# A four-layer graph network on one core: one-hot products in place of a gather, marks moved to another engine, a fused subtraction

## The chip, the cores and the metric

The kernel runs on one core of one Trainium2 chip. The metric is the device time of one execution in microseconds (us), as the median of several runs. A profile is one further execution, recorded by the hardware profiler; its times are microseconds, and those of single instructions are nanoseconds (ns). The engines of the core are TensorE (PE in the profile, with its weight loads as PEld), VectorE (DVE), ScalarE (ACT), GpSimd (POOL) and the queue of SyncE (SP), which here only starts transfers.

## The reference, cut to what matters

There are 16 graphs of 1024 nodes with 64 features each. Four layers follow one another, each of the form x = x + f(relu(layernorm(x)), adj). Layers 0, 1 and 3 multiply by the weighted adjacency matrix. Layer 2 is the costly one: for every node and every feature it takes the 0.25, 0.5 and 0.75 quantiles over the node's neighbours (after a rule that removes some neighbours), adds them with weights 0.25, 0.5 and 0.25, and puts the sum through a small network:

```python
h = maximum(layernorm(x), 0)
valid = dilate(adj, mask) > 0                    # which neighbours count
agg = sum(w * quantile(h over the valid neighbours, t)
          for t, w in ((.25, .25), (.5, .5), (.75, .25)))
y = relu((h + agg) @ W1 + b1) @ W2 + b2
x = x + y * mask
```

The layernorm is (x - mean(x)) / sqrt(var(x) + 1e-5) over the 64 features.

## The kernel before, in words

A graph's 1024 nodes lie on 128 partitions in 8 blocks. The main path is `direct_path`. It sorts the nodes of each graph by their number of neighbours, so that blocks of nodes with similar counts share one sorting network. The position of each node in this order is `pos`, and the node at each position is `node`. Six streams work on the graphs:

- `adjacency` loads the adjacency matrix, transposes it on TensorE, counts and removes neighbours, writes a matrix of keys to DRAM, and works out `pos` and `node` (L1062 to L1085).
- `layers` computes layers 0 and 1 and the normalised input `h2` of layer 2, and writes it to DRAM as the table `h_d`. Layers 0 and 1 each hold a product of 16 instructions with the transposed adjacency (`messages`, L883); layer 1 is followed by eight in-place copies on ScalarE (L1228) that sum the degrees.
- `neighbour_lists` fetches the rows of keys in sorted order with indirect transfers (L1100), finds the neighbours with max-of-eight instructions on VectorE (L1119, L1133), and makes the lists `index`.
- `gathers` fetches the features of the neighbours from `h_d` with one indirect transfer for each slot and block (L1294), 124 a graph, into the tiles `raw0` to `raw4`, one for each group of blocks, of which there is a single buffer each.
- `sorts` runs the sorting networks on VectorE (L1327), adds up the weighted quantiles in `agg` (L1344 to L1350), and sends `agg` to DRAM from SP's queue (L1355). The order of its rows is the sorted one.
- `tail` brings the aggregate back into the order of the nodes: eight indirect transfers on GpSimd read the rows of `agg_d` at `pos` into `res` (L1366). `paired` then adds `h2` and `res` while it transposes them on TensorE (L891), ScalarE copies the sum (L893), and the rest of layer 2 (L1375 to L1381) and layer 3 (L1403 to L1419) follow.

The order of all instructions is fixed when the program is built. A planner in Python holds a clock for each engine (`clk.dve`, `clk.pe`, `clk.act`, `clk.pool`), to which each piece of work adds planned costs. A stream gives the time from which it wants to continue; the planner takes the first stream of the list whose time has come by `clk.dve`. `after` adds to the clocks and returns when a result should be there. Each engine then works through its own list strictly in order, so a waiting instruction holds up everything behind it on that engine.

`gate` (L919 to L926) ties GpSimd to this plan. It is called ahead of every few gathers. If more than 3 us of planned VectorE time have gone since the last mark, a one-element memset is issued on VectorE (L923), and GpSimd copies that element (L925); so GpSimd doesn't go on before VectorE has reached the mark.

`preln` (L850 to L865) is the layernorm, used four times a graph: a sum (L854), its scaling to a mean (L855), the subtraction (L856), a square on ScalarE (L857), a second sum (L859), a root on ScalarE (L860), a reciprocal (L862), a multiplication (L863), and a relu on ScalarE (L864).

The pool `lists` has two buffers of every tile unless said otherwise. Tiles with one tag share these buffers.

Of the kernel before, what the change touches and what calls it, by code (L numbers as in the profile page):

```python
# [7 lines left out]
F32 = mybir.dt.float32  # L8
F16 = mybir.dt.float16
BF = mybir.dt.bfloat16  # L10
I32 = mybir.dt.int32
# [3 lines left out]
ALU = mybir.AluOpType  # L15
AX = mybir.AxisListType

P = 128
C = 64
NB = 8  # L20
N = 1024
# [30 lines left out]
J_ID, J_BIG, J_OFF, J_ST, J_ROW, J_ONE, J_PI, J_NI, J_NEG, J_END = 0, 128, 256, 384, 896, 1920, 2048, 2176, 2184, 2312  # L52
# [680 lines left out]
def direct_path(ctx: ExitStack, tc: tile.TileContext, t: dict, out: bass.AP, flag):  # L733
# [3 lines left out]
    nc = tc.nc  # L737
    x_in, adj, nodemask = t["x"], t["adj"], t["nodemask"]
    B = x_in.shape[0]

    const = ctx.enter_context(tc.tile_pool(name="const", bufs=1))
    loads = ctx.enter_context(tc.tile_pool(name="loads", bufs=2))
    graph = ctx.enter_context(tc.tile_pool(name="graph", bufs=1))
    nodes = ctx.enter_context(tc.tile_pool(name="nodes", bufs=2))
    lists = ctx.enter_context(tc.tile_pool(name="lists", bufs=2))
# [10 lines left out]
    ch = const.tile([P, J_END], F16, name="eh")  # L756
# [4 lines left out]
    stair, pidx = ch[:, J_ST:J_ST + N // 2], ch[:, J_PI:J_PI + P]  # L761
    nid = ch[:, J_NI:J_NI + NB]
    jrow, onerow = ch[0:1, J_ROW:J_ROW + N], ch[0:1, J_ONE:J_ONE + P]
# [45 lines left out]
    nc.gpsimd.dma_start(mask8, nodemask.rearrange("b (i p) -> (b i) p", p=P))  # L809
    maskf = lists.tile([B * NB, P], F32, tag="ab", name="maskf")  # L810
    nc.vector.tensor_copy(maskf, mask8)
# [10 lines left out]
    clk = Clock()  # L822

    def after(dve=0.0, pe=0.0, act=0.0, lat=0.3):

        clk.dve += dve
        at = clk.dve
        if pe:
            clk.pe = at = max(clk.pe, at) + pe
        if act:  # L830
            clk.act = at = max(clk.act, at) + act
        return at + lat

# [15 lines left out]
    def preln(u, x, ha):  # L849

        s = nodes.tile([P, 4, NB], F32, name="stat")
        xc = mid(u, [P, NB, C])
        sq = mid(u, [P, NB, C])
        nc.vector.tensor_reduce(s[:, 0], x, AX.X, ALU.add)  # L854
        ts(s[:, 1], s[:, 0], 1.0 / C, None, op0=ALU.mult)  # L855
        tt(xc, x, s[:, 1, :, None].to_broadcast([P, NB, C]), ALU.subtract)  # L856
        act(sq, xc, AF.Square)  # L857
        yield after(1.5, act=0.65, lat=1.2)
        nc.vector.tensor_reduce(s[:, 2], sq, AX.X, ALU.add)  # L859
        act(s[:, 3], s[:, 2], AF.Sqrt, bias=eps, scale=1.0 / C)  # L860
        yield after(0.7, act=1.0, lat=1.5)
        nc.vector.reciprocal(s[:, 2], s[:, 3])  # L862
        tt(xc, xc, s[:, 2, :, None].to_broadcast([P, NB, C]), ALU.mult)  # L863
        act(ha[:, :, :C], xc, AF.Relu)  # L864
        yield after(0.9, act=0.65)  # L865
# [20 lines left out]
    def paired(hs, dst):  # L886

        p = bank()
        for q in range(4):
            for e, h in enumerate(hs):  # L890
                nc.tensor.matmul(p[:, q * P:(q + 1) * P], h[:, 2 * q:2 * q + 2, :].rearrange("p u c -> p (u c)"), identf,  # L891
                                 start=e == 0, stop=e == len(hs) - 1)
        nc.scalar.copy(dst, p)  # L893
        clk.pe = max(clk.pe, clk.dve) + 2.0 * len(hs)
        clk.act = max(clk.act, clk.pe) + 0.7
# [15 lines left out]
    def even(v, u):  # L911

        return v.rearrange("c (q u p) -> c u q p", u=2, p=P)[:, u]


    marks = []
    slots = const.tile([1, 8], F32, name="mark")
    opened = const.tile([1, 2], F32, name="gate")

    def gate():  # L920
        if not marks or clk.dve > marks[-1] + 3.0:
            k = len(marks)
            nc.vector.memset(slots[:, k % 8:k % 8 + 1], 0.0)  # L923
            clk.dve += 0.15
            nc.gpsimd.tensor_copy(opened[:, k % 2:k % 2 + 1], slots[:, k % 8:k % 8 + 1])  # L925
            marks.append(clk.dve)  # L926

# [13 lines left out]
    def adjacency(b):  # L941
# [108 lines left out]
        for q in range(2):  # L1050
            spread = lists.tile([P, 4, P], F32, tag="ab", name="spread")
            tt(spread, identf[:, None, :].to_broadcast([P, 4, P]),
               key[:, 4 * q:4 * q + 4, None].to_broadcast([P, 4, P]), ALU.mult)
            nc.tensor.matmul(p[:, q * 512:(q + 1) * 512], onesf, spread.rearrange("p j m -> p (j m)"),
                             start=True, stop=True)
        over = nodes.tile([P, NB], F32, name="over", bufs=1)
        for i in range(NB):
            sink = lists.tile([P, N], F16, tag="ab", name="sink")
            act(sink, p, AF.Sign, bias=neg[:, i:i + 1], accum_out=over[:, i:i + 1])
        yield after(1.6, pe=1.3, act=10.5, lat=2.0)  # L1060
        pos = nodes.tile([P, NB], I32, name="pos", bufs=5)
        ts(pos, over, 0.5, 511.5, op0=ALU.mult, op1=ALU.add)  # L1062
# [5 lines left out]
        nc.vector.tensor_copy(ph, pi)  # L1068
        low = lists.tile([P, NB, P], F16, tag="ab", name="low")
        tt(low, pidx[:, None, :].to_broadcast([P, NB, P]), ph[:, 0, :, None].to_broadcast([P, NB, P]), ALU.is_equal)  # L1070
# [13 lines left out]
        node = nodes.tile([P, NB], I32, name="node", bufs=3)  # L1084
        nc.vector.tensor_copy(node, p[:, :NB])  # L1085
        clk.dve += 0.1
        g.update(pos=pos, node=node, m=m, keys_d=keys_d)
        done.add(("keys", b))
# [222 lines left out]
    def sorts(b):  # L1311
        g = state[b]
        agg_d = dram.tile([N, C], F32, name="agg_d")
        agg = nodes.tile([P, NB, C], F32, name="agg", bufs=1)
        for k, (b0, n, cap, low, *_) in enumerate(GROUPS):
# [18 lines left out]
            o = sum(len(_wanted(kk, ll)) * m for _, m, kk, ll, *_ in GROUPS[:k])  # L1334
            wv = g["wts"][:, o:o + len(places) * n].rearrange("p (q i) -> p q i", i=n)

            half = nodes.tile([P, C], F32, name="half", bufs=1)
# [15 lines left out]
            yield clk.dve  # L1353
        yield clk.dve + 2
        nc.sync.dma_start(agg_d.rearrange("(i p) c -> p i c", p=P), agg)  # L1355
        g.update(agg_d=agg_d, agg_at=clk.dve + 4)
        done.add(("sorts", b))


    def tail(b):  # L1360
        g = state[b]
        x, ha, adjt_d = g["x"], g["h2"], g["adjt_d"]
        yield g["agg_at"]
        res = nodes.tile([P, NB, C], F32, name="res", bufs=1)
        for i in range(NB):
            nc.gpsimd.indirect_dma_start(res[:, i, :], None, g["agg_d"],  # L1366
                                         bass.IndirectOffsetOnAxis(ap=g["pos"][:, i:i + 1], axis=0))
        clk.pool = max(clk.pool, clk.dve) + 10.5
        yield clk.pool + 3.5
        rt = mid(1, [P, 512])  # L1370
        paired((ha, res), rt)
        h1 = big(1, [P, N])
# [4 lines left out]
        y = per_node(bank(), h1, w22, 8, b22)  # L1377
        yield after(0, pe=6.5, act=2.1) + 6.0
        o = mid(1, [P, NB, C])
# [51 lines left out]
    programs = [_program(*group[2:]) for group in GROUPS]  # L1431
    edge = lists.tile([1, 2, C], F32, tag="ab", name="edge")
    nc.vector.memset(edge[:, 0], 0.0)
# [64 lines left out]
def _constants():  # L1498
# [25 lines left out]
    eh[p, J_ST + p] = 2050  # L1524
    eh[0, J_ROW:J_ROW + N] = np.arange(N) - 2047
    eh[0, J_ONE:J_ONE + P] = 1
# [76 lines left out]
```

## Time and profile before

| what | value |
|---|---|
| time, median of 3 runs | 3631.67 us (3631.34 to 3632.71) |
| time of the profiled execution | 3640.35 us |
| its span | 3638.5 us |
| VectorE busy | 3072.9 us, 84% of the span |
| GpSimd busy | 2651.7 us, 73% |
| TensorE busy | 1993.7 us, 55% |
| ScalarE busy | 1410.6 us, 39% |
| mean granted TensorE clock | 0.698 of full speed |

The span is the time from the first to the last recorded instruction. Dispatch of an instruction isn't counted as busy, so an engine with many short instructions is fuller than its busy share says; between two indirect transfers GpSimd shows an idle time "<-issue" of about 0.3 us. A row of the groups gives the line, the engine and operation, output <- inputs with shapes, the count, then busy time in us, mean duration in ns, and the idle time in front of these instructions with what ended it. A row of waits gives who waited for whom: the total in us, how many times, and the longest. One product with fp32 operands leaves two matmul records.

### The profile page before, as it was taken

The page shows a single profiled execution, that of the slowest core. Times are in us where ns is not written, and L with a number is a line of the kernel's source. Part 1 is how long each engine was busy: PE and PEld are TensorE (multiplying, and loading weights), DVE is VectorE, ACT ScalarE, POOL GpSimd, SP SyncE. Part 2 cuts the span into 40 slices and gives each one's busy share as a digit, 9 for nine tenths or more (in the row PEclk, how much of TensorE's full clock was granted, in tenths as well). Part 3 has the DMA queues.
Part 4 walks back from the last instruction along what each step waited for, and adds up shares of the span by engine and source line. Part 5 has one row for each costly group of instructions (what it writes and reads, how often), then busy time and mean ns, then how long its engine had stood idle before and what let it go on. Part 6 is the DMA issues. An engine that isn't in the chain of part 4 may idle for free.

```text
span 3638.5 us, 31082 instructions
## 1 busy us (share of the span) xinstructions
PE 1993.7 (55%) x7587; PEld 923.9 (25%) x7587; DVE 3072.9 (84%) x7539; ACT 1410.6 (39%) x2770; POOL 2651.7 (73%) x2777
## 2 busy tenths in 40 slices
PE   6564565746666565746555556765646565550303
PEld 3222222323222222322222222232322322220101
DVE  3497989989898998989798997989898888989662
ACT  5444434344444344353444435443443534330000
POOL 1187787878777787877777787787778777777881
PEclk9676767676676676767676667667667776765555
DMA  2324243342424334151433425243332525232211
GB/s 90 120 62 122 60 129 102 112 129 62 152 66 133 95 109 128 49 184 44 145 81 111 122 72 166 55 134 89 126 109 63 167 56 157 49 123 52 74 27 57
DMA packets 237344, 362.38 MB, mean 100 GB/s; under 512 B 126848, under 2 KB 128496, under 8 KB 237152
## 3 DMA queue, kind: packets, MB, share of 16 engines
q1 hardware_dynamic: 156912, 255.00, 20.2%
q0 software_dynamic: 80096, 104.70, 14.1%
q8 instruction: 62, 1.02, 0.1%
q14 instruction: 130, 1.06, 0.1%
q10 hardware_dynamic: 144, 0.59, 0.0%
HBM read 245.30 MB, written 114.81 MB: 99 GB/s over the span
## 4 chain that ended last, share of the span: by engine, by line
DVE 61%; POOL 11%; issue 11%; DMA 7%; PE 5%; ACT 3%; SPq 0%; DVEq 0%; POOLq 0%; ACTq 0%
DVE raw L1327 16%; DVE other L1327 16%; POOL raw L1294 10%; DVE most L1133 6%; PE pt L883 4%; DVE found L1119 4%; DMA raw<-h_d,index 3%; DVE agg L1346 2%; ACT adjt L1228 2%; DMA k<-keys_d,node 2%; DVE k L1128 2%; DVE nb L948 2%; DVE found L1134 1%; DVE k L1130 1%; DVE gone L1007 1%
## 5 line engine op out<-in xcount | busy, mean ns | idle before, releaser
L1294 POOL DMA_INDIRECT raw<-h_d,index x1984 | 2165.2, 1091 | 558.8 <-issue 498.8
L1327 DVE TENSOR_TENSOR other<-raw 128x512 f32<-128x512 f32 (+11 forms) x816 | 536.4, 688 | 162.5 <-DMA raw<-h_d,index 132.9
L883 PE MATMUL pt<-adjt,ha 128*65 128x512 f32 (+1 forms) x1024 | 492.7, 643 | 91.0 <-DVE ha L1215 68.7
L995 PE MATMUL pt<-eh,nbt 128*128 128x512 f16 (+3 forms) x1024 | 236.6, 379 | 310.2 <-ACT nbt L984 309.7
L1327 DVE TENSOR_TENSOR raw<-other 128x512 f32<-128x512 f32 (+10 forms) x464 | 356.7, 791 | 5.6
L955 PE MATMUL pt<-ef,a 128*128 128x128 f32 x1024 | 205.2, 356 | 220.2 <-ACT adjt L957 136.2
L925 POOL COPY gate<-mark 1x1 f32<-1x1 f32 x462 | 156.4, 339 | 225.0 <-DVE mark L923 217.3
L1133 DVE MAX8 most<-k 128x8 uint16<-128x1024 uint16 x208 | 255.4, 1228 | 7.2
L962 ACT ACTIVATE nb<-nb 128x512 f16<-128x512 f16 x256 | 159.2, 624 | 255.6 <-DVE nb L948 149.6
L883 PEld LDWEIGHTS pt<-adjt,ha 128*65 128x65 f32 (+1 forms) x1024 | 149.9, 150 | 417.6 <-issue 403.3
L955 PEld LDWEIGHTS pt<-ef,a 128*128 128x128 f32 x1024 | 155.6, 183 | 321.6 <-ACT adjt L957 173.9
L995 PEld LDWEIGHTS <-nbt 128*128 128x128 f16 x1024 | 110.4, 120 | 436.0 <-ACT nbt L984 340.7
L1327 DVE TENSOR_TENSOR raw<-other,raw 128x640 f32<-128x640 f32 (+3 forms) x448 | 216.5, 494 | 5.0
L884 ACT COPY big<-pt 64x1024 f32<-64x1024 f32 (+1 forms) x32 | 32.3, 1008 | 476.8 <-PE pt L883 476.8
L1327 DVE TENSOR_TENSOR raw<-raw,other 128x128 f32<-128x128 f32 (+7 forms) x496 | 211.7, 436 | 6.0
L1403 PE MATMUL tm<-at,ha 128*64 128x512 f32 x512 | 175.3, 786 | 74.5 <-DMA at<-adjt_d 74.5
L1002 ACT ACTIVATE gone<-pt,sf 128x512 f16<-128x512 f32 x256 | 161.4, 683 | 124.5 <-DVE sf L976 95.3
L1029 PE MATMUL pt<-eh,gone 128*128 128x128 f16 x1024 | 127.2, 253 | 145.2 <-DVE gone L1007 77.8
L1327 DVE TENSOR_TENSOR other<-other,raw 128x128 f32<-128x128 f32 (+4 forms) x448 | 200.6, 459 | 3.8
L1119 DVE MAX8 found<-k 128x8 f32<-128x1024 f16 x128 | 156.3, 1221 | 51.6 <-DMA k<-keys_d,node 51.6
L891 PE MATMUL pt<-ef,res 128*128 128x128 f32 x128 | 38.9, 399 | 291.9 <-DMA res<-agg_d,pos 291.9
L1034 ACT ACTIVATE nb<-pt 128x1024 f16<-128x1024 f32 x120 | 122.4, 1020 | 164.9 <-PE pt L1032 89.2
(192 smaller groups left out, 4373.6 us busy)
## 6 DMA issues: line engine op xcount, KB each, us to landing
a<-in_adj_dram SPq DMA_DIRECT2D x64, 1024.0 KB
adjt_d<-adjt SPq DMA_DIRECT2D x64, 1024.0 KB
at<-adjt_d SPq DMA_DIRECT2D x128, 512.0 KB
keys_d<-nb SPq DMA_DIRECT2D x64, 512.0 KB
raw<-h_d,index POOLq DMA_INDIRECT x1984
x<-in_x_dram SPq DMA_DIRECT2D x16, 256.0 KB
h_d<-h SPq DMA_DIRECT2D x16, 256.0 KB
agg_d<-agg SPq DMA_DIRECT2D x16, 256.0 KB
```

Source lines behind the costliest of these rows:

```text
L883: nc.tensor.matmul(p[p0:p0 + n, s], h[:, j, :n], adjt[:, j, s], start=j == 0, stop=j == NB - 1)
L925: nc.gpsimd.tensor_copy(opened[:, k % 2:k % 2 + 1], slots[:, k % 8:k % 8 + 1])
L955: nc.tensor.transpose(p[:, u * P:(u + 1) * P], a[:, j * P:(j + 1) * P], identf)
L962: act(nb[:, i, s], nb[:, i, s], AF.Copy, accum_out=mn[:, q, i:i + 1])
L995: nc.tensor.matmul(p[:, o:e], nbt[:, j, :], stair[:, :e - o], start=j % 4 == 0, stop=j % 4 == 3 and j != i)
L1002: act(gone[:, i, s], p[:, s], AF.Abs, bias=sf[:, 2 + q, i:i + 1], scale=2.0)
L1029: nc.tensor.matmul(p[:, d], gone[:, j, i * P:(i + 1) * P], big_i, start=False, stop=j == 4 * q + 3 and i // 4 != q)
L1119: nc.vector.max(out=eights[0], in_=src)
L1133: nc.vector.max(out=most, in_=less.bitcast(U16))
L1294: nc.gpsimd.indirect_dma_start(raw[:, s, i * C:(i + 1) * C], None, h_ds[b % 3], bass.IndirectOffsetOnAxis(ap=g["index"][:, at:at + 1], axi ...
L1327: tt(view(two[to], *((i, vi) if greater else (j, vj)), w), view(two[s], i, vi, w), view(two[u], j, vj, w), ALU.max if greater else ALU.min)
L1403: nc.tensor.matmul(p[q * C:(q + 1) * C, :], ha[:, j, :], even(ats[j], q), start=j == 0, stop=j == NB - 1)
```

## The change

Three parts are changed, and one rearrangement of buffers goes with them.

*Marks.* A mark is now a one-element copy on ScalarE. It is issued inside `after`, whenever work on ScalarE has been planned and more than 3 us of planned ScalarE time have gone since the last mark; its planned time is kept. `gate` issues no mark any more: it looks among the last 20 marks for the latest with a planned time more than 1 us before GpSimd's, and, unless that one was used before, lets GpSimd copy it.

*Aggregate.* `agg` stays in SBUF. From the positions a tile `place` is kept (the node's number less 2047, as the row `iota` counts). `tail` builds for each of the 8 blocks two 128x512 matrices `hot` on VectorE, which hold 1 where the number of the column's node equals that of the row's. TensorE multiplies the block of `agg` by them and adds into one PSUM tile, which already holds the transposed `h2`. ScalarE copies the sum. `sorts` of a graph now waits, in the plan, until the aggregate of the graph before has been brought back.

*Layernorm.* The scaling of the sum and the subtraction become one instruction, x + sum * (-1/64).

*Buffers.* The tiles of tag "ab" share the buffers of "nbt"; `pos` has one buffer instead of five, and `place` has five.

```diff
+    def mark():
+        if not marks or clk.act > marks[-1][0] + 3.0:
+            t = slots[:, len(marks) % 32:len(marks) % 32 + 1]
+            nc.scalar.copy(t, eps[:1])
+            clk.act += 0.2
+            marks.append((clk.act, t))
+
+    def gate():
+        due = [m for m in marks[-20:] if m[0] < clk.pool - 1.0]
+        if due and gates[-1:] != due[-1:]:
+            gates.append(due[-1])
+            nc.gpsimd.tensor_copy(opened[:, len(gates) % 2:len(gates) % 2 + 1], due[-1][1])
...
     def after(dve=0.0, pe=0.0, act=0.0, lat=0.3):
...
             clk.act = at = max(clk.act, at) + act
+            mark()
         return at + lat
...
-        ts(s[:, 1], s[:, 0], 1.0 / C, None, op0=ALU.mult)
-        tt(xc, x, s[:, 1, :, None].to_broadcast([P, NB, C]), ALU.subtract)
+        nc.vector.scalar_tensor_tensor(xc, s[:, 0, :, None].to_broadcast([P, NB, C]), -1.0 / C, x, op0=ALU.mult, op1=ALU.add)
...
-    def gate():
-        if not marks or clk.dve > marks[-1] + 3.0:
-            k = len(marks)
-            nc.vector.memset(slots[:, k % 8:k % 8 + 1], 0.0)
-            clk.dve += 0.15
-            nc.gpsimd.tensor_copy(opened[:, k % 2:k % 2 + 1], slots[:, k % 8:k % 8 + 1])
-            marks.append(clk.dve)
...
-            spread = lists.tile([P, 4, P], F32, tag="ab", name="spread")
+            spread = lists.tile([P, 4, P], F32, tag="nbt", name="spread")
...
+        place = nodes.tile([P, NB], F32, name="place", bufs=5)
+        ts(place, p[:, :NB], -2047.0, None, op0=ALU.add)
...
     def sorts(b):
...
+            while b and ("back", b - 1) not in done:
+                yield None
...
-        yield clk.dve + 2
-        nc.sync.dma_start(agg_d.rearrange("(i p) c -> p i c", p=P), agg)
-        g.update(agg_d=agg_d, agg_at=clk.dve + 4)
+        g.update(agg=agg)
...
     def tail(b):
...
-        yield g["agg_at"]
-        res = nodes.tile([P, NB, C], F32, name="res", bufs=1)
-        for i in range(NB):
-            nc.gpsimd.indirect_dma_start(res[:, i, :], None, g["agg_d"],
-                                         bass.IndirectOffsetOnAxis(ap=g["pos"][:, i:i + 1], axis=0))
-        clk.pool = max(clk.pool, clk.dve) + 10.5
-        yield clk.pool + 3.5
+        yield clk.dve + 1.0
+
+        agg = g["agg"]
+        p = psum.tile([P, 512], F32, name="tm")
+        for q in range(4):
+            nc.tensor.matmul(p[:, q * P:(q + 1) * P], ha[:, 2 * q:2 * q + 2, :].rearrange("p u c -> p (u c)"), identf,
+                             start=q == 0, stop=False)
+        clk.pe = max(clk.pe, clk.dve) + 2
+        for k in range(NB):
+            for u in range(2):
+                hot = lists.tile([P, 512], F32, name="hot")
+                ts(hot.rearrange("p (q m) -> p q m", m=P), even(iota, u), g["place"][:, k:k + 1], None, op0=ALU.is_equal)
+                nc.tensor.matmul(p[u * C:(u + 1) * C, :], agg[:, k, :], hot, start=False, stop=k == NB - 1)
+            yield after(0.8, pe=1.5) - 1.5
+        done.add(("back", b))
         rt = mid(1, [P, 512])
-        paired((ha, res), rt)
+        nc.scalar.copy(rt, p)
...
-        yield after(0, pe=6.5, act=2.1) + 6.0
+        yield after(0, pe=6.5, act=3.2) + 6.0
...
-    eh[0, J_ROW:J_ROW + N] = np.arange(N) - 2047
+    eh[:, J_ROW:J_ROW + N] = np.arange(N) - 2047
```

## The prediction

> **What bounds the kernel now.** I read the page's busy shares first, then the same by slices and by stages (busy time in windows), then who waited for whom on VectorE and GpSimd, in the steady stretch from 440 to 3300 us and at the end, and last the rows of the operations concerned. Busy shares of the page, and two of its rows of 40 slices of 91 us:
>
> ```profile
> PE 1993.7 (55%) x7587; PEld 923.9 (25%) x7587; DVE 3072.9 (84%) x7539; ACT 1410.6 (39%) x2770; POOL 2651.7 (73%) x2777
> ...
> DVE  3497989989898998989798997989898888989662
> POOL 1187787878777787877777787787778777777881
> ```
>
> VectorE (DVE) is the busiest, with a slow start and end. By windows (us, then PE, PEld, DVE, ACT, POOL, clock, DMA share, GB/s), one steady window of about one graph, and a late one:
>
> ```profile
> 1320.00:1540.00 220.00, 133.95 (x487) 60.15 (x488) 198.26 (x490) 88.85 (x175) 173.27 (x179) 0.71 0.36 103
> ...
> 3300.00:3400.00 100.00, 3.61 (x12) 2.79 (x12) 69.95 (x194) 2.46 (x7) 78.64 (x85) 0.50 0.20 46
> ```
>
> In the steady window VectorE works 198 of 220 us. GpSimd shows 173, but it is really as full: the waits of GpSimd from 440 to 3300 us (total, times, longest) are
>
> ```profile
> POOL raw L1294 <- issue: 419.2, 1487, 3.1
> POOL gate L925 <- DVE mark L923: 83.7, 47, 6.4
> ```
>
> The first is 0.28 us of dispatch before each gather, so it is work, not slack: 173 + 179 x 0.28 = 223 us of a 220 us window, within its roughness. Real slack is the 84 us at the gates, 6 us a graph (the transfers of agg to DRAM lie 212 us apart, so the stretch holds 13.5 graphs). So two engines are full together, VectorE at 90% and GpSimd at about 95%, and each now and then waits for the other. VectorE's waits in the same stretch:
>
> ```profile
> DVE other L1327 <- DMA raw<-h_d,index: 46.6, 13, 10.4
> DVE found L1119 <- DMA k<-keys_d,node: 45.3, 9, 11.2
> DVE stat L862 <- ACT stat L860: 44.6, 4, 18.1
> DVE stat L859 <- ACT mid L857: 28.1, 5, 9.7
> DVE other L1327 <- issue: 15.2, 4, 6.2
> ```
>
> Lines 1, 2 and 5 (the last is a sort's first step too) are gathers that come late: 107 us, 7.9 a graph. Lines 3 and 4 are ScalarE behind a long product on TensorE: 73 us, 5.4 a graph. From 3300 us on GpSimd alone bounds; its waits there:
>
> ```profile
> POOL raw L1294 <- issue: 39.4, 148, 0.3
> POOL res L1366 <- DMA agg_d<-agg: 22.7, 1, 22.7
> ```
>
> It never stands still until the last aggregate is in DRAM, while VectorE waits 68.5 us for raw.
>
> **What the Trainium skill says.** *VectorE: DVE Perf Modes*, "The perf-mode tier table": an instruction with one source in SBUF doubles its rate with 4-byte data and reaches four times with 16-bit data, while one with two sources in fp32 stays at one element a cycle. The trace agrees: 1024 elements with one source take 0.70 us (f32 to f16) and 0.49 (f16 to f16), with two fp32 sources 1.22. *GPSIMD Engine Reference*, its table of properties: the SBUF interfaces are shared with VectorE, with contention when VectorE runs in a two-port mode or has two SBUF inputs. The trace agrees in kind: a gather takes 0.94 us while VectorE rests and up to 2.03 while it sorts.
>
> **The change, part by part.** The rows I price from (busy, mean ns):
>
> ```profile
> L948 DVE TENSOR_SCALAR nb<-a 128x1024 f16<-128x1024 f32 x128 | 90.1, 704 | 14.7 <-DMA a<-in_adj_dram 14.6
> L1007 DVE TENSOR_SCALAR gone<-gone,sf 128x1024 f16<-128x1024 f16 x112 | 54.9, 490 | 30.0 <-ACT gone L1002 30.0
> L923 DVE MEMSET mark<- 1x1 f32 x462 | 26.9, 59 | 0.0
> L1366 POOL DMA_INDIRECT res<-agg_d,pos x128 | 135.5, 1059 | 62.8 <-issue 34.4 <-DMA agg_d<-agg 22.7 <-PE pt L907 1.8
> L1403 PE MATMUL tm<-at,ha 128*64 128x512 f32 x512 | 175.3, 786 | 74.5 <-DMA at<-adjt_d 74.5
> ```
>
> *One-hots on VectorE, added.* 16 a graph, 256 in all, 128x512 f32 from f16 with a scalar per partition. No such row exists. L1007 with its scalar operand moves 1024 elements in 490 ns at four a cycle; 512 at two a cycle take the same, 490 ns. Neighbouring short steps overlap: L1346 lasts 277 ns, but starts come every 195 in the timeline, so 0.08 less: 0.41 us, 256 x 0.41 = +105 us. Bounds: four a cycle 0.28 (+72), one a cycle 0.68 (+174). I take two, since the output is 4 bytes wide. (In a two-port mode they also press on GpSimd's gathers, as the sorts do already: 105 us of such pressure beside 3073.) The step that makes "place" reads 8 columns of PSUM: 16 x 0.2 = +3.
>
> *Marks.* 462 memsets leave VectorE: −27 us (0 if all sat in bubbles between dependent sorts, −60 with the 0.09 to 0.3 us from start to start). ScalarE gets marks instead: about 45 planned ScalarE steps a graph, those less than 3 us apart skipped, so about 30 x 16 = 480 copies of 0.16 us (128x8 copies take 164 ns) = 80 us on an engine 39% busy; hidden there, and without that cover 5 us a graph. A gate costs GpSimd 0.34 busy less the 0.14 of dispatch that it hides = 0.2 us; in the steady stretch I expect as many gates as now, at the end few, as ScalarE has little planned there.
>
> *Layernorm.* 64 steps of 0.18 us go with the bubble after them, 0.28 from start to start in the timeline at 3595.2: 0.24 x 64 = −15 us. The fused step with a scalar should take the 691 ns of the other two-source steps of 512 (L1239), as the subtraction does.
>
> VectorE in all: 105 + 3 − 27 − 15 = +66 us, 4.1 a graph, all on a bound engine.
>
> *Gathers of res, removed.* 128 x (1.06 + 0.28) = −171 us of GpSimd, 10.7 a graph; the 16 transfers of agg leave SP's queue. TensorE no longer stands in front of them (64 us in the steady stretch).
>
> *Products, added.* 16 a graph like L1403, which has two records to a product: 175.3/256 = 0.68 us each, 11 us a graph, less 2.4 for res. TensorE goes from about 61% to 65% of the steady stretch. The new wait: only two hot tiles, so the third one-hot waits for the first product, behind what TensorE has queued, with all of VectorE's sorts behind it. The planner's pacing, about 1.1 us or more from pair to pair, keeps step with products of 1.1 to 1.4 us a pair; I allow 1 us a graph, with 0 and 8 as ends. The sorts also wait in the plan for the previous "back", which comes 15 to 25 us after its sorts, before the next group of sums is wanted.
>
> *Shared tiles* (tag "ab" into "nbt") follow each other in one stream; covered by the key phase's own order, a few tenths a graph otherwise.
>
> *What moves.* With 10.7 us a graph of air on GpSimd, I let 70% of the late gathers go: −75 us. Steady sum: 13.5 x 4.1 = +55, −75, +13 for the new wait: −7. End, GpSimd alone: eight gathers for graph 14 at 1.25 us = −10, some 27 gates at 0.16 = −4. Last tail: now from the last sum at 3568.9 over DRAM and eight gathers to ScalarE's copy at 3584.7, 15.8 us; new, eight pairs at about 1.7 us (one-hot, product, next one-hot into the same tile), 13.6: −2. In all −23 us against the profiled 3640.35 us (span 3638.5 and 1.85 around it). The runs' median is 3631.67, 8.7 lower, so I carry the difference over: **3609 us**.
>
> **Rivals.** *Full relief:* all 107 us go and TensorE's freer queue halves the waits for ScalarE (−36), new wait nil: 55 − 107 − 36 − 16 = −104 at best, −70 as its middle: 3562. For it: GpSimd is what is late in three of five waits. Against: the sums keep VectorE at 92%, so some meeting points stay. *Gates hold GpSimd:* the mark in "layers" is issued after eight in-place copies (L1228, 1.04 us each), though planned before them, so it comes 8.3 us late once a graph; gathers gated on it stand and the late gathers stay: 55 + 13 − 16 = +52, 3684. It decides once such stalls eat more than about 8 of the 10.7 us. *TensorE holds VectorE (slower):* at 1905 us, when a sort ends, TensorE is busy until 1917 and then waits for ScalarE until 1922. If the one-hots of each graph wait 8 us there rather than 1, 13.5 x 7 = +95: 3704; from 2.7 us a graph on, the gain is gone. For it: two buffers, queues in order. Against: TensorE mostly waits for VectorE's results. *One element a cycle:* +69 more, 3678.
>
> **Chances.** Likeliest 0.43 (own range 3585 to 3635), full relief 0.14, gates 0.17, TensorE 0.18, slow one-hots 0.08. 0.2% (7 us) is about what runs of this kernel can tell from nothing. Of the likeliest case I put 0.36 below 3624 and 0.07 within; with full relief that makes faster 0.50. Of the other three (0.43) 0.02 falls within, by their mild ends: same 0.09, slower 0.41. Range 3560 to 3700: from the middle of full relief to short of the worst of TensorE's case.
>
> **What would show it.** Right: 256 one-hots near 0.49 us and no mark row on VectorE; GpSimd without res; VectorE's waits for raw and k in 440 to 3300 near 30 us, waits for the product at the one-hot near 13; starts of the back-products about 211 us apart; the last sort some 14 us sooner relative to its graph's first gather. Wrong: one-hots of 0.7 us or more, VectorE waiting on TensorE for over 40 us there, or gates waiting on ScalarE for over 100 us with raw still late.

## The result, and the profile after

| | before | after |
|---|---|---|
| median of 18 runs each | 3631.57 us | 3645.07 us |
| profiled execution | 3640.35 us | 3647.31 us |
| its span | 3638.5 us | 3645.5 us |

The ratio is 1.0034, with a 95% interval of 1.0025 to 1.0044: the changed kernel is slower by 0.34%, some 12 us (13.5 between the medians). The prediction was 3609 us, faster. The time is inside the range and the sign is wrong.

The page of the changed kernel, busy shares and two rows of the 40 slices:

```profile
PE 2185.3 (60%) x7971; PEld 939.4 (26%) x7971; DVE 3164.4 (87%) x7285; ACT 1451.8 (40%) x3277; POOL 2503.6 (69%) x2553
...
DVE  3596998899899999989989999998999899998983
POOL 1177776858768686876868677686867868686770
```

VectorE does 91 us more than before, where the prediction's sum said 66, and GpSimd 148 us less. VectorE is denser at the end (the last slices), and GpSimd falls to 6 or 5 in 14 of the 40 slices, where it had 7 and 8 between start and end. The same two stretches by windows (us, then PE, PEld, DVE, ACT, POOL, clock, DMA share, GB/s):

```profile
1320.00:1540.00 220.00, 143.03 (x527) 60.44 (x524) 204.33 (x470) 94.60 (x212) 160.97 (x169) 0.74 0.37 101
3300.00:3400.00 100.00, 41.57 (x138) 17.23 (x136) 88.07 (x192) 26.54 (x56) 63.33 (x63) 0.69 0.44 127
```

The single prices came out as expected. Groups of instructions, with count, busy time, mean ns, and idle time in front:

```profile
L1381 DVE TENSOR_SCALAR hot<-eh,place 128x512 f32<-128x512 f16 x256 | 114.6, 488 | 36.1 <-PE tm L1382 35.8
...
L832 ACT COPY mark<-cols 1x1 f32<-1x1 f32 x507 | 88.5, 175 | 0.4
...
L841 POOL COPY gate<-mark 1x1 f32<-1x1 f32 x366 | 122.7, 335 | 23.1 <-ACT mark L832 21.4
```

The one-hot takes 488 ns (490 was taken), there are 507 marks of 175 ns (480 of 160), and 366 gates (462 before). The price of the marks that left VectorE did not come out. The 462 memsets of the kernel before show 26.9 us of busy time, but all except 0.2 us of it lies inside the time of other instructions of VectorE. A piece of that kernel's timeline (start, us, instruction):

```profile
1943.39 0.22 DVE L1327 TENSOR_TENSOR raw<-other 128x64 f32<-128x64 f32 x1
1943.41 0.06 DVE L923 MEMSET mark<- 1x1 f32 x1
1943.65 0.41 DVE L1327 TENSOR_TENSOR other<-other 128x192 f32<-128x192 f32 x1
```

The memset runs inside the step ahead of it, and the step behind it starts no later for it. At 423 of the marks the same two neighbours also follow each other elsewhere in this trace without a mark; on average they start at the same distance, to less than 1 ns. So VectorE got nothing for the marks, where the prediction took 27 us off. The one-hots add 97 us of busy time of their own (105 taken).

The larger part of the miss is in the waits. VectorE's, from 440 to 3300 us (total, times, longest):

```profile
DVE other L1334 <- DMA raw<-h_d,index: 53.0, 18, 6.1
DVE hot L1381 <- PE tm L1382: 27.4, 15, 4.4
DVE stat L878 <- ACT mid L876: 26.3, 17, 2.4
DVE found L1127 <- DMA k<-keys_d,node: 19.8, 12, 4.1
DVE agg L1353 <- PE tm L1382: 18.1, 12, 3.0
DVE other L1334 <- DMA k<-keys_d,node: 12.7, 2, 8.6
```

Lines 1, 4 and 6 are the late gathers: 85.5 us, where 107 stood before and about 32 were expected. Lines 2 and 5 are the new wait for TensorE, 45.5 us. Line 3 is ScalarE, 26 us in place of 73. And GpSimd's waits in the same stretch, the changed kernel first and then two lines of the kernel before:

```profile
POOL k L1108 <- DVE found L1142: 174.4, 13, 14.4
POOL packed L1287 <- DMA pack<-pack_d: 39.2, 9, 6.2
POOL packed L1287 <- issue: 30.6, 30, 5.2
...
POOL gate L841 <- ACT mark L832: 15.6, 9, 6.1
POOL k L1108 <- DVE place L1093: 13.9, 5, 6.1
```

```profile
POOL k L1100 <- DVE found L1134: 5.2, 7, 3.4
POOL packed L1279 <- issue: 11.1, 37, 0.3
```

The first line is the finding. GpSimd stands 174 us before a fetch of key rows, once a graph and up to 14.4 us at a time, for VectorE's search for neighbours (5.2 us before). With `packed`, which waits for a list made from the same search, and `place`, it is 258 us; the gates fell from 84 to 16.

A stretch of fixed length always gains as much idle time as it loses work, so the cost of the change has to be counted over the same graphs. The 13 graphs from the first sort of the second to that of the fifteenth, before and after (columns as above):

```profile
422.02:3185.31 2763.29, 1648.44 (x6297) 758.69 (x6296) 2484.81 (x6102) 1171.36 (x2291) 2137.99 (x2219) 0.71 0.37 106
...
426.46:3215.33 2788.87, 1765.32 (x6416) 753.86 (x6416) 2553.37 (x5883) 1178.59 (x2652) 2034.01 (x2065) 0.72 0.36 102
```

They take 25.6 us longer, 2.0 a graph. GpSimd is busy 104 us less and issues 154 instructions fewer, 43 us of dispatch at 0.28: a relief of 147 us, 11.3 a graph. In the same graphs its waits before the fetches of keys, before `packed` and at the gates grew from 109 to 274 us, by 12.6 a graph. **All the time that GpSimd was relieved of, and a little more, it stands.**

Over the whole: the first sort of the first graph starts at 208.3 us (207.5 before). From there to that of the fifteenth graph it is 3007.0 us (2977.8), +29. From there to the end of the span it is 430.2 (453.2), −23. In all +7 in the profiled pair.

### Where the wait comes from

The fetches of key rows have four buffers (`k`), so the fifth of a graph must wait until VectorE has finished with the first block. What matters is where in GpSimd's order the fetches stand. The timeline of GpSimd in the changed kernel (start, us, instruction, idle time in front):

```profile
1859.15 0.95 POOL L1302 DMA_INDIRECT raw<-h_d,index  x1 [0.30 <-issue]
1860.40 0.94 POOL L1108 DMA_INDIRECT k<-keys_d,node  x1 [0.30 <-issue]
1861.65 0.95 POOL L1108 DMA_INDIRECT k<-keys_d,node  x1 [0.30 <-issue]
1862.91 1.70 POOL L1108 DMA_INDIRECT k<-keys_d,node  x1 [0.30 <-issue]
1864.91 1.56 POOL L1108 DMA_INDIRECT k<-keys_d,node  x1 [0.30 <-issue]
1878.96 0.95 POOL L1108 DMA_INDIRECT k<-keys_d,node  x1 [12.50 <-DVE found L1142]
```

and of the kernel before, near the same time:

```profile
1806.95 1.50 POOL L1100 DMA_INDIRECT k<-keys_d,node  x1 [0.16 <-issue]
1808.76 0.95 POOL L1100 DMA_INDIRECT k<-keys_d,node  x1 [0.30 <-issue]
1810.01 1.22 POOL L1100 DMA_INDIRECT k<-keys_d,node  x1 [0.30 <-issue]
1811.53 0.94 POOL L1100 DMA_INDIRECT k<-keys_d,node  x1 [0.30 <-issue]
1812.78 1.00 POOL L1294 DMA_INDIRECT raw<-h_d,index  x1 [0.30 <-issue]
```

Before, after four fetches come more gathers of the current graph, and the fifth fetch follows at 1828.8 us without a wait. After, the line at 1859.15 is the last gather of the graph, so nothing is left to do between the fourth and the fifth. Counted in the traces: how many of the 124 gathers of a graph GpSimd has issued when the first fetch of the next graph's keys comes, over the last thirteen graphs. The kernel before, the changed one and the one without gates were traced on chips where the kernel before takes some 3630 us, the other four on slower ones (below):

```
kernel                      gathers issued before the first fetch       GpSimd's idle time before
                                                                        the fifth fetch, 12 graphs
before                      113 113 105 105 97 97 93 81 81 64 64 72 64     4 us
marks alone                 113 105 105 105 93 100 97 93 81 89 89 81 77    4
layernorm alone             as before                                      4
aggregate alone             124 in every graph                           131
after                       124 in every graph                           166
after, gathers of res back  117 to 124                                    83
after, without gates        124 in every graph                           131
```

(A plain dispatch of 0.3 us each is 4 us.) It closes into a loop, measured on graphs 5 to 14 of the changed kernel. From the fifth fetch to the end of the graph's last gather GpSimd needs 194.6 us. 3.4 us later the sort of the last group starts; it had waited for that gather 3.6 us a graph on average. VectorE's search in the next graph's first block follows that sort's first steps, and 16.4 us after the sort's start the next fifth fetch goes out. The sum is 214.5 us, the period. Such a sum closes by construction; that this loop sets the period is read from the waits, which stand at both handovers: GpSimd waits for VectorE at the fetch, and VectorE for GpSimd at the last sort.

Two more traces of the changed kernel, from slower chips (below), close the same loop, again over graphs 5 to 14: 209.7 + 4.1 + 16.4 = 230.2 us, and 213.5 + 3.4 + 16.4 = 233.3 us. The instructions of every engine stand in the same order in all three traces. Only GpSimd's part of the loop is longer, and its gates wait longer there, from 440 to 3300 us:

```profile
POOL gate L841 <- ACT mark L832: 172.4, 33, 12.5
...
POOL gate L841 <- ACT mark L832: 199.7, 41, 11.8
```

### The profile page after: what moved, and what is told of

It reads as the page before. It is cut to its first block, busy times and chain, and to the rows that moved or that the text cites. A ratio compares the mean times of both kernels' runs of the same rounds, so it can differ in the third digit from the quotient of the medians.

```text
span 3645.5 us, 31708 instructions
## 1 busy us (share of the span) xinstructions
PE 2185.3 (60%) x7971; PEld 939.4 (26%) x7971; DVE 3164.4 (87%) x7285; ACT 1451.8 (40%) x3277; POOL 2503.6 (69%) x2553
## 4 chain that ended last, share of the span: by engine, by line
DVE 45%; PE 17%; POOL 14%; DMA 8%; ACT 8%; issue 7%; DVEq 0%; ACTq 0%; SPq 0%; POOLq 0%
POOL raw L1302 12%; DVE raw L1334 11%; DVE other L1334 11%; PE pt L902 7%; DVE most L1141 5%; DMA raw<-h_d,index 4%; DVE found L1127 3%; ACT adjt L1236 3%; DMA k<-keys_d,node 2%; ACT sink L1065 2%; DVE hot L1381 2%; PE tm L1382 2%; DVE agg L1355 2%; DVE nb L954 1%; PE pt L1035 1%
## 5 line engine op out<-in xcount | busy, mean ns | idle before, releaser
L1302 POOL DMA_INDIRECT raw<-h_d,index x1984 | 2191.0, 1104 | 560.2 <-issue 516.9
L902 PE MATMUL pt<-adjt,ha 128*65 128x512 f32 (+1 forms) x1024 | 472.6, 622 | 22.2 <-DVE ha L1223 20.9
L1001 PE MATMUL pt<-eh,nbt 128*128 128x512 f16 (+3 forms) x1024 | 251.1, 395 | 314.9 <-ACT nbt L990 314.9
L1108 POOL DMA_INDIRECT k<-keys_d,node x128 | 128.8, 1006 | 386.4 <-DVE found L1142 210.2
L1382 PE MATMUL tm<-hot,agg 128*64 128x512 f32 x512 | 212.0, 768 | 261.1 <-DVE hot L1381 261.1
L1418 PE MATMUL tm<-at,ha 128*64 128x512 f32 x512 | 191.2, 844 | 79.3 <-DMA at<-adjt_d 79.3
L961 PEld LDWEIGHTS pt<-ef,a 128*128 128x128 f32 x1024 | 147.1, 178 | 329.7 <-ACT adjt L963 190.1
L1065 ACT ACTIVATE sink<-pt,neg 128x1024 f16<-128x1024 f32 x128 | 140.5, 1122 | 64.4 <-PE pt L1060 64.4
```

What stands on the lines that cost most here:

```text
L902: nc.tensor.matmul(p[p0:p0 + n, s], h[:, j, :n], adjt[:, j, s], start=j == 0, stop=j == NB - 1)
L961: nc.tensor.transpose(p[:, u * P:(u + 1) * P], a[:, j * P:(j + 1) * P], identf)
L1001: nc.tensor.matmul(p[:, o:e], nbt[:, j, :], stair[:, :e - o], start=j % 4 == 0, stop=j % 4 == 3 and j != i)
L1302: nc.gpsimd.indirect_dma_start(raw[:, s, i * C:(i + 1) * C], None, h_ds[b % 3], bass.IndirectOffsetOnAxis(ap=g["index"][:, at:at + 1], axi ...
L1382: nc.tensor.matmul(p[u * C:(u + 1) * C, :], agg[:, k, :], hot, start=False, stop=k == NB - 1)
L1418: nc.tensor.matmul(p[q * C:(q + 1) * C, :], ha[:, j, :], even(ats[j], q), start=j == 0, stop=j == NB - 1)
```

## The experiments

In the runs of the first three groups the kernel before itself took 3763 to 3841 us, against 3632 on the first chip. The traces from these chips show waits that no record of the profile explains. Ratios there are taken to the kernel before on the same chip, are compared with others of the same chip alone, and are not carried over to the chip of the result, which I call the first. Where an expectation speaks of a first chip, it means the one on which each part ran alone.

### Each part alone

Marks, layernorm, the aggregate with its buffers, and marks with layernorm, each put into the kernel before (the edits are the parts of the diff shown).

> Only the marks part: the kernel before with its marks copied on ScalarE instead of set on VectorE. Theory A (VectorE's own work sets the period, so work taken from it comes off the time): 27 us less of VectorE work give 15 to 27 us less time. Theory B (the chain adjacency, keys, lists, gathers sets the period, and VectorE's work is mostly room beside it): the time stays within 7 us. Theory C (gates on ScalarE's marks hold GpSimd): GpSimd's waits at the gates rise above 150 us in 440 to 3300 us and the kernel gets slower by 10 us or more.

> Only the layernorm part: the kernel before with the fused subtraction. Theory A: 12 to 18 us less VectorE work, 8 to 15 us less time. Theory B: within 7 us.

> Only the aggregate part, with the shared tiles: the kernel before with the one-hot products, marks on VectorE and layernorm in two steps as before. Theory A: the whole change lost 12 us although marks and layernorm gained about 30, so this part alone is about 40 us slower than before. Theory B: marks and layernorm gave nothing, so this part alone is 5 to 20 us slower, through TensorE's queue held at the one-hots.

> Marks and layernorm without the aggregate part, which stays with the gathers of the kernel before. Theory A: 25 to 40 us faster than before, 35 to 50 us faster than the whole change. Theory B: within 7 us of before.

Measured beside 3840.76 us: marks 1.0128 [1.006, 1.0195]; layernorm 1.0035 [1.0008, 1.0061]; aggregate 1.0084 [1.0057, 1.0111]; marks with layernorm 1.0114 [1.0036, 1.0192].

No part is faster there. With the marks alone, the gates waited 206 us from 440 to 3300 us, which was to be the sign that marks on ScalarE hold GpSimd. But with the layernorm alone, where VectorE still sets the marks, they waited 190 us on the same chip, so this sign tells nothing here. The aggregate alone is 28 us slower, between what the two theories said.

What the traces tell of the order holds for any chip, since it is fixed in the program: only the aggregate moves the fetches behind the last gather. GpSimd's waits in that kernel, 440 to 3300 us:

```profile
POOL k L1103 <- DVE found L1137: 138.9, 15, 14.2
```

while marks with layernorm has 15.1 us there. The kernel with the aggregate alone has no gathers of `res` either, and it isn't faster.

### The same with the whole, on one chip

> The whole change itself, as the reference for the runs beside it. The earlier runs stood on a chip where the kernel before took 3833 to 3841 us, with waits on TensorE, ScalarE and VectorE that no record explains. If this chip gives about 3632 us for the kernel before, the whole change should be at 1.003 of it; if it gives about 3835 again, theory D (a change of chip costs the whole change more, as its ScalarE marks and TensorE products stand behind those waits) says 1.015 to 1.02.

> The aggregate part alone, again. If VectorE's own work sets the period, about 40 us slower than before; otherwise 0 to 20 us slower (on the first chip 1.008 of before).

> Marks and layernorm without the aggregate part, again. If VectorE's own work sets the period, 25 to 40 us faster than before. If not, within 7 us of before, or slower by as much as gates on ScalarE's marks hold GpSimd (on the first chip 1.011 of before).

> The whole change with the transfer of agg to DRAM and the eight gathers of res kept beside the products, again. If GpSimd's relief is worth what the prediction said, 50 to 85 us slower than the whole change; if GpSimd's free time only goes into standing at the key gathers, less than 20 us.

The last has the whole change, and brings the aggregate back a second time by the old way, with `pos` in five buffers again; nothing reads it:

```diff
+        nc.sync.dma_start(agg_d.rearrange("(i p) c -> p i c", p=P), agg)
...
         done.add(("back", b))
+        res = nodes.tile([P, NB, C], F32, name="res", bufs=1)
+        for i in range(NB):
+            nc.gpsimd.indirect_dma_start(res[:, i, :], None, g["agg_d"],
+                                         bass.IndirectOffsetOnAxis(ap=g["pos"][:, i:i + 1], axis=0))
+        clk.pool = max(clk.pool, clk.dve) + 10.5
```

Measured beside 3763.49 us: the whole 1.0341 [1.0275, 1.0407], the aggregate alone 1.0194 [1.0136, 1.0252], marks with layernorm 1.0193 [1.0151, 1.0234], the whole with `res` back 1.0455 [1.0417, 1.0493].

The two halves add up to 3.9%, near the 3.4% of the whole. The aggregate alone costs 59 us here, more than either outcome of its expectation. Giving GpSimd its 171 us back costs 60 us, about a third. That lies within the 50 to 85 us that the expectation gave to the prediction's term, and above the 20 us of a mere standstill: on this chip a part of the relief was worth time. The wait before the fifth fetch is halved (155 to 85 us over 12 graphs).

The run doesn't isolate GpSimd's work, though. The planned time of the gathers changes the order on VectorE as well: in this trace the last sort of a graph starts 35 us after its last gather, not 4 as in the whole, and the next fifth fetch goes out 27 us ahead of that sort. So this kernel doesn't go through the loop above.

### One cost at a time on the whole

A third one-hot buffer; the gathers of `res` back; a second pass of ScalarE for the positions (`adjacency`, every other block); and 79 us more work for VectorE (two spare products after each sort but that of the first group).

```diff
-                hot = lists.tile([P, 512], F32, name="hot")
+                hot = lists.tile([P, 512], F32, name="hot", bufs=3)
```

```diff
+            if i % 2:
+                sink = lists.tile([P, N], F16, tag="nbt", name="sink")
+                act(sink, p, AF.Sign, bias=neg[:, i:i + 1], accum_out=over[:, i:i + 1])
-        yield after(1.6, pe=1.3, act=10.5, lat=2.0)
+        yield after(1.6, pe=1.3, act=15.7, lat=2.0)
```

```diff
+            for _ in range(2 if k else 0):
+                tt(spare, identf[:, None, :].to_broadcast([P, 4, P]), onesf[:, None, :].to_broadcast([P, 4, P]), ALU.mult)
+                clk.dve += 0.62
+                yield clk.dve
...
+    spare = const.tile([P, 4, P], F32, name="spare")
```

> The whole change with a third hot tile; the order on every engine stays the same, only the wait of a one-hot for the product two before it goes. Theory A (VectorE's own work and waits set the period): most of the 36 us that VectorE waits at the one-hots comes off, 15 to 35 us less than the whole change. Theory B (the chain adjacency, keys, lists, gathers sets the period): VectorE waits elsewhere instead, within 8 us of the whole change.

> The whole change, with the transfer of agg to DRAM and the eight gathers of res kept beside the products; nothing reads res. It puts back what GpSimd was relieved of (171 us in all) and nothing else. The prediction's term: relief was worth 75 us in the steady stretch and 10 at the end, so this is 50 to 85 us slower than the whole change. Theory B: GpSimd only stands at the key gathers 11 us less per graph, and the time rises by less than 20 us, at the end only.

> The whole change with four of the eight comparisons on ScalarE that give the positions (sink, 1.1 us each with its accumulator) issued twice: 5.2 us more per graph on ScalarE between the keys and the lists, 83 us in all, nothing more on VectorE. Theory B: 45 to 85 us slower than the whole change. Theory A: less than 20 us slower.

> The whole change with eight more two-source steps of 128x512 per graph on VectorE (two after each sort but the first, into a tile that nothing reads), planned as 0.62 us each: 5 us a graph, 79 us in all. Theory A: 60 to 85 us slower than the whole change. Theory B: less than 30 us slower, VectorE's waits shrinking instead.

and, with the whole change beside them on a third chip,

> The whole change, as the reference for the three runs beside it: 1.003 of the kernel before on an undisturbed chip, up to 1.034 where the kernel before takes 3760 us or more.

> The whole change with eight more steps of 128x512 per graph on VectorE, 79 us of work in all, beside its own reference. Theory A (VectorE's own work sets the period): 60 to 85 us slower than the whole change. Theory B (the stream adjacency, whose end starts the lists and so GpSimd's gathers, sets it): less than 30.

> The whole change with 83 us more on ScalarE inside the stream adjacency, nothing more on VectorE. Theory B: 45 to 85 us slower than the whole change. Theory A: less than 20.

> The whole change with the eight gathers of res kept, 171 us of GpSimd's time. The prediction's term says 50 to 85 us slower than the whole change; if GpSimd's free time only goes into waiting for the first list, less than 20.

| | beside 3833.12 us | beside 3776.41 us |
|---|---|---|
| the whole | – | 1.0416 [1.0357, 1.0475] |
| third one-hot buffer | 1.0197 [1.0147, 1.0247] | – |
| 79 us more on VectorE | 1.019 [1.0148, 1.0232] | 1.0291 [1.024, 1.0341] |
| second pass on ScalarE | 1.0264 [1.0206, 1.0322] | 1.0396 [1.0341, 1.045] |
| `res` back on GpSimd | 1.0327 [1.0274, 1.0381] | 1.0533 [1.0483, 1.0584] |

The chip of the right column has the whole beside the others. There 79 us more work on VectorE took nothing away; the kernel was even 30 us faster. So the amount of VectorE's work doesn't set the period on that chip. It doesn't show that such work is free in the order of the whole: the planned time moved VectorE's instructions, and the next fifth fetch goes out 53 us ahead of the last sort's start rather than 16 us after it, outside the loop. The 83 us more for ScalarE in `adjacency` left the time as it was, with the loop still closed, at 232.9 us; so that stream doesn't set it by its ScalarE work. GpSimd's work costs about a third of itself again (52 us of 171), in the changed order described above.

The third buffer has no run of the whole beside it, so its time tells nothing of the wait at the one-hots. Its order is that of the whole, and its loop takes 232.4 us, between the 230.2 and 233.3 of the whole on two other slow chips; no gain from the buffer shows in that.

### Without the gates, and a control

After this what remained was GpSimd in the loop. The gates lie in it, 24 a graph. One kernel leaves out both calls of `gate`, and changes nothing else; the marks stay.

```diff
-        gate()
         for i in range(KB):
             load_keys(i)
...
-                if s % (4 // n) == 0 and s < PLACES[b0]:
-                    gate()
```

The control changes one planned latency in the kernel before, from 0.3 to 0.35 us (the default of `after`), so that the planner orders the work otherwise with nothing added or removed.

> The whole change without any gate on GpSimd (the marks on ScalarE stay, nothing waits for them). Where the kernel before takes 3760 us or more, GpSimd waits some 200 us at the gates of the whole change, against 23 on an undisturbed chip. If these waits are what the change loses there, 30 to 70 us faster than the whole change, 1.015 to 1.03 of before. If GpSimd only waits elsewhere instead, 1.034 to 1.042 of before as for the whole change.

> A control: the kernel before with one planned latency changed from 0.30 to 0.35 us, so that no work, wait or buffer is added or taken away, and only the planner's order of the instructions differs. If the order written out by the planner moves the time by chance, the ratio to before lies off 1 by 0.3% or more, either way; if not, within 0.2%.

Measured on a chip where the kernel before took 3628.74 us, so that neither outcome of the expectation, which speaks of slower chips, applies: without gates 3563.95 us, 0.9816 [0.9796, 0.9836]; the control 3627.4 us, 0.9995 [0.9987, 1.0003].

The control's other order is worth nothing: the first fetch of keys stands after 81 to 93 gathers in its last nine graphs (64 to 97 in the kernel before), and the time is the same. The changed kernel without its gates is 1.8% faster than the kernel before. Beside the 3645 us of the changed kernel that is 81 us less, with the kernel before within 3 us on the two chips. In the traces every engine has its instructions in the same order as in the changed kernel; only the 366 gates are missing, so the gates are the whole difference. Its span is 3556.8 us. VectorE's waits in it, 440 to 3300 us, the four that answer to those of after:

```profile
DVE found L1126 <- DMA k<-keys_d,node: 14.8, 14, 2.7
DVE agg L1350 <- PE tm L1379: 14.4, 12, 2.4
DVE hot L1378 <- PE tm L1379: 12.8, 15, 3.7
...
DVE other L1331 <- DMA raw<-h_d,index: 1.6, 4, 0.6
```

and GpSimd's:

```profile
POOL k L1108 <- DVE found L1141: 153.9, 16, 11.6
POOL k L1108 <- DVE place L1093: 64.6, 12, 9.2
```

The late gathers went from 85.5 us to 20 (lines 1 and 4, 1.0 for k and 2.8 of dispatch at a sort's start), the wait for TensorE from 45.5 to 27. The same 13 graphs take 70 us less than in the changed kernel, nearly all of it these late gathers. GpSimd still stands before the fetches, longer even, but it now meets the last sort in time: in the loop its part is 187.0 us instead of 194.6, the last sort doesn't wait at all, and the period is 209.3 us. This loop no longer has a wait at its second handover; VectorE, busy for 94% of the stretch, is now the fuller by far. The 7.6 us are more than the price of the gates: each costs 0.335 us less about 0.14 of dispatch that it hides, 0.2 us, so 24 make 4.7, and they waited 1.2 us a graph. The rest, 1.7, is not assigned.

What isn't settled: why the planner puts the fetches behind the last gather. The marks, the layernorm and a changed latency don't do it. The shared buffers can't, as no buffer enters the planner's clocks or the conditions on which its streams go on. With the planned 10.5 us of `res` back the fetches come only a little earlier (117 to 124). Left are the plan's new wait of `sorts` for the previous aggregate and the 6.4 us a graph that `tail` now adds to the clock of VectorE; they were not tried apart. No run puts the fetches back among the gathers with the rest of the change in place, so what their place alone costs is read from the waits and not measured. Nor was the kernel before run without gates, so how the 1.8% splits between the change and the missing gates is open.

## Why the prediction was wrong

| step of the prediction, us a graph | said | measured over 13 graphs |
|---|---|---|
| VectorE's work | +4.1 | +5.3 |
| late gathers | −5.6 | −1.5 |
| wait at one-hots and sums for TensorE | +1.0 | +3.3 |
| waits for ScalarE | 0 | −4.2 |
| waits for loads of the adjacency and x | 0 | −0.7 |
| sum of the rows | −0.5 | +2.1 |
| time from graph to graph | | +2.0 |
| end, in all (last two graphs; the prediction from 3300 us on) | −16 | −23 |

**The step that failed** is under "What moves": "With 10.7 us a graph of air on GpSimd, I let 70% of the late gathers go: −75 us." Over the 13 graphs 19 us of 105 went. The prediction took the air as time by which the gathers come earlier. The trace shows it as a standstill of 13 us a graph before the fifth fetch of key rows, at a point where GpSimd has nothing else to do, and the gathers of the last groups, at the far end of the loop, stayed as late as they were. What they lack is time on GpSimd inside that loop: with only the gates gone, the late gathers fall to 20 us. The prediction priced what each stream adds and removes, but took GpSimd's order as given; that the fetches of keys would move to the end of it appears in no step and no rival. With −5.6 in place of −1.5, the sum would be −2.0 a graph and the forecast's sign would have held.

**VectorE's work** was mis-sized too, by 1.2 us a graph. The memsets, 1.7 us a graph in its sum, took no time of their own. The prediction had named this end of its range ("0 if all sat in bubbles between dependent sorts").

**The new wait for TensorE** was right as a mechanism and too small: 45.5 us from 440 to 3300, 3.4 a graph, where 1 was allowed. It is two waits: 27.4 at the one-hots, and 18.1 at the first sum (L1353), which waits for the last product of the graph before because `agg` has one buffer; the second was not seen. The prediction's own signs for this came true: over 40 us in all, and over 2.7 us a graph, from where "the gain is gone". With +1.0 instead of +3.3 the graphs would take about as long as before. Without the gates 27 us of it are left, 2.0 a graph, and that kernel is faster.

**ScalarE's waits** fell by 4.2 us a graph; the forecast left them unchanged, and no run tells why they fell. That was luck: by the rows above, the changed kernel would without it be slower by some 60 us more (an estimate, 14 graphs of 4.2). Of the rival *full relief* that half came true ("halves the waits for ScalarE"). Its first half, the late gathers, needed the gates gone. Its time of 3562 us is near the 3564 of the kernel without gates by chance, as 20 us of late gathers and 27 us of waits for TensorE remain in that kernel.

**Gates hold GpSimd** named the right part for the wrong reason. The late mark behind the eight copies is not seen: the gates wait 16 us in the whole stretch, the longest 6.1. They matter through their own time in a loop without slack.

**One-hots, marks, layernorm.** A one-hot of 512 elements takes 488 ns, as long as 1024 elements of L1007 (490): half the rate of an instruction with 2-byte data on both sides. The Trainium skill, *VectorE: DVE Perf Modes*, "The perf-mode tier table", gives this step from four times to two for one source with 16-bit and with 4-byte data, and the trace agrees (the one-hot reads the first and writes the second). The marks on ScalarE are covered. The fused subtraction takes 693 ns, as taken. That it is worth 15 us isn't shown: alone it measured 1.0035 on another chip.

Two readings of the prediction are off without weight: the longest gather of the kernel before takes 2.58 us, not 2.03, and TensorE is busy for 59% of the steady stretch, not 61.

**End.** The gathers of the last graph and the tail: right in kind, −23 for −16, though not over quite the same stretch. VectorE's longest wait for raw there fell from 25.7 us to 12.3.

## What to carry to other kernels

When work is taken from an engine that runs in order, ask what its next instruction will wait for. The time freed can turn into a wait at the first instruction that depends on the other busy engine, as it did here; it helps only if other work stands in between. Where a planner sets the order, the change also moves instructions that it doesn't touch. Compare their positions before pricing (here the fetch of keys, which stood after 64 to 113 of the 124 gathers and now stands after all).

Ask whether an instruction has time of its own before counting its removal as a gain; the memsets had none. Small ties between engines, 0.2 us each, cost their whole time in a loop that has no slack; whether the same ties were free before wasn't measured. And count the cost of a change over the same pieces of work, since in a stretch of fixed length work and idle time always add up to the same.

## What the runs showed of the hardware

- A one-element memset between two other instructions of VectorE cost it no time: 462 of them, of 59 ns each, added 0.2 us of busy time.
- The copy of one element on GpSimd is uneven: 177 ns at least, 226 in the median, 1266 at most, 335 on average over 366.
- In the kernel before, a gather took 0.95 us on average where VectorE ran nothing beside it (164 of them), and 1.17 where it mostly ran sorting steps (1000).
- The kernel before took 3629 to 3841 us in the median, depending on the chip. The changed kernel took 3645, 3879 and 3920 us with the same instructions in the same order in its traces. The traces of the slower chips show waits of VectorE without a record that ends them, and GpSimd's gates wait about 200 us there, with the marks on VectorE as on ScalarE. On one of these chips 79 us more work on VectorE, in another order, made the kernel 30 us faster. The cause of the slower chips is open.
